# Conditional layer of a fused transformer block: weights standing in array quarters, transposes through the DMA queue of ScalarE, token tiles spread over the long phases

## The chip, the cores and the metric

The kernel runs on one core of a Trainium2 chip. The metric is the device time of one execution in microseconds (us); the lower the better. A time of a kernel is the median of several runs. Beside the times there is one profiled execution, from which all the views below come.

## The reference

The input x is 64 sequences of 64 rows with 1024 columns; 4096 rows in all, called tokens here. The computation is a block of four layers with two residual sums:

```python
W = weights[condition]                       # 16 matrices of 64 x 64, one picked per sequence
y = jnp.einsum('bct,bcd->bdt', x, W)         # conditional layer: mixes the 64 rows of a sequence
x = x + attention(y)                         # 32 heads of 32, qkv projection, softmax over 64, out projection
x = x + ffn(cond2(x))                        # routed low-rank layer, then a quantized gated feed-forward
```

The change concerns the first line alone: for each sequence b, y[b] is the transpose of its 64x64 weight times x[b]. Everything is in float32, apart from the quantized part at the end.

## The kernel before, in words

The kernel has three stages. `attention` does the conditional layer, the qkv projection, scores, softmax and context; the output projection and the second residual stage follow. The change lies in `attention`, which takes about the first 1430 us.

**Blocks and phases.** The 4096 tokens are worked in NBLK = 8 blocks of 512. A block is four tiles of 128 tokens (PB = 4); one tile holds two sequences. For every block the conditional layer's result is kept transposed (columns of x on the partitions), as four quarters named B11, B12, B21, B22 (first index: half of the columns; second: half of the tokens), and from them four differences T1 to T4. These are the operands of a Winograd form of the matrix product, which makes each projection from seven products instead of eight (`Winograd.ORDER` is 1, 6, 7, 5, 2, 4, 3). The projections of a block are four chunks c of query (`psq`) and key (`psk`) rows, seven products of about 1.73 us each, and two groups g of values (`psv`), seven products of 3.45 us each. The work of a block is cut into four phases, one per chunk c. In a phase the scores, the softmax and the context of chunk c are made, while TensorE is filled with the projections of the next chunk ("fills"). Phase 0 holds the query fill, the second values group and the key fill; phases 1 and 2 a query and a key fill; phase 3 the conditional layer of the next block, its first values group and its first query and key fill. So phases 0 and 3 are the long ones.

**Scores to context.** A phase starts two groups of scores (`group`), each of two units u; unit (m, t) is a quarter of the block. A group's 32 passes run on 64x64 quarters of TensorE's array (line 498). The key operand lies in four tiles kbd0 to kbd3, one per unit; kbd1 is written by ScalarE from product 2 (line 419), the others by VectorE (line 421). After the softmax (lines 510 to 522) a unit's probabilities are split into two planes of 16 bits (`parted`, line 528, ScalarE: tile ph), turned by a DMA transpose that SyncE issues (`turned`, line 533: phT), joined again (`joined`, line 540, ScalarE: pT), and used as operand of the context (`context`, line 550). The context's results lie in the PSUM pool `ps_c` of two banks, from which ScalarE copies them (line 561) and sends them away by its own DMA queue (line 562).

**The order of the work.** Each engine works its instructions in the order in which the program issues them, and a semaphore wait holds back all that stands behind it on the same engine. The order is planned by hand: `run` issues a product, lets a clock `now` of planned time go on by its cost, and `at(time, f)` puts a step into a heap from which `run` takes what is due. `rest` parts of products (the copies out of PSUM) are issued one product later (`behind`). `phase` places the two groups at the start and the middle of the phase's planned length. `with_sums` hangs extra VectorE or GpSimd work before a product.

**The conditional layer before** (`conditional`, lines 342 to 381). For a tile j, x is loaded by SyncE (`load_x`, line 246; four at a time for the next block, pool `xp` of 4 buffers), the two 64x64 weights are gathered by GpSimd (line 248) and copied (line 380) into the diagonal of a 128x128 tile `wbd`. TensorE then takes each 128x128 piece of x as the standing operand and streams wbd (line 355): eight matmuls a tile, each two passes in float32, 64 passes a block. This gives y already transposed, in banks of `ps_g` (4 buffers, shared with the projections). VectorE and ScalarE copy in turn (lines 361 and 363) into the quarters; lines 371 and 376 make the T tiles. All of it stands at the start of phase 3, ahead of the products that read it.

**Weights.** Query and key weights are loaded by SyncE into two buffers (line 295, 1.8 MB each): when a projection's last product is issued, the load for the projection after the next one follows. Value weights are seven tiles of 0.5 MB, each loaded after its last use (line 299). `chores`, line 112 and after, prepare weights of the later stages on the side.

Of the kernel before, what the change touches and what calls it, by code (L numbers as in the profile page):

```python
# [182 lines left out]
def attention(tc, a, x_t, ctx_d, ident, dram, ps_g, KC, PB, NBLK, NCH, HPC, H, C, chores, early, op):  # L183
# [27 lines left out]
    with ExitStack() as ctx, ExitStack() as mid:  # L211
# [11 lines left out]
        yp = pool(mid, "y1", 1, side="right")  # L223
        p1 = pool(mid, "p1", 1, side="right")
        w = pool(early, "w1", 1)
        xp = pool(early, "xp", 4)


        cond_i = w.tile([P, KC * 4], I32, tag="cond_i", name="cond_i")
# [6 lines left out]
        nc.vector.tensor_copy(row_f, row_i)  # L236
        nc.vector.tensor_scalar(idx, cond_i, float(C), row_f, ALU.mult, ALU.add)

        def load_x(b):
            tiles = []  # L240
            for j in range(PB):
                i = b * PB + j
                xt = xp.tile([P, H], F32, tag="x", name=f"x_{i}")
                if i == PB - 1:
                    held(xt[:, 0:1], tiles[0][0])
                nc.sync.dma_start(xt, x_t[i])
                wg = xp.tile([P, C], F32, tag="wg", name=f"wg_{i}")
                nc.gpsimd.indirect_dma_start(
                    out=wg[:, :],
                    out_offset=None,  # L250
                    in_=cw,
                    in_offset=bass.IndirectOffsetOnAxis(ap=idx[:, i:i + 1], axis=0),
                )
                tiles.append((xt, wg))
            return tiles

        def held(word, other):


            nc.scalar.copy(word, other[:, 0:1])  # L260
# [24 lines left out]
        def load_qk(b, wh, c, eng=None):  # L285
            t = w_qk[b, wh, c] = wp.tile([P, 7, KQ, P], F32, tag="wqk", name=f"w{wh}_{b}_{c}")
            if b == 0:
                if (wh, c) == ("q", 0):
                    held(t[:, SLOT["A11"], 0, 0:1], x_next[0][1])
                for key in RAW:  # L290
                    nc.sync.dma_start(t[:, SLOT[key], :, :], quarter(key, (0 if wh == "q" else H) + c * P, P))
                return sums(
                    eng or nc.vector, lambda key: t[:, SLOT[key], :, :], lambda: nc.gpsimd.dma_start(qk_d[wh, c], t)
                )
            nc.sync.dma_start(t, qk_d[wh, c])
# [18 lines left out]
            return sums(eng, at, stored)  # L314

        bqkv = act.tile([P, 3 * KC], F32, tag="bqkv", name="bqkv")
        x_next = load_x(0)
        first_sums = load_qk(0, "q", 0) + load_qk(0, "k", 0, nc.gpsimd)
        nc.sync.dma_start(bqkv, a["qkvb_t"])
        first_sums += load_v_raw(0, nc.gpsimd)  # L320
# [1 line left out]

        wbd = []
        for j in range(PB):
            t = w.tile([P, P], F32, tag=f"wbd{j}", name=f"wbd{j}")
            nc.vector.memset(t, 0.0)
            wbd.append(t)
        kbd, vbd = [], []  # L330
        for u in range(4):
            t = act.tile([P, 2, HB], F32, tag=f"kbd{u}", name=f"kbd{u}")
# [6 lines left out]

        B = {}  # L340

        def conditional(b, tiles):

            def one(hf, j):
                key = f"B{hf + 1}{j // 2 + 1}"
                box = []

                def product():
                    xt = tiles[j][0]
                    if j % 2 == 0:  # L350
                        B[key] = yp.tile([P, KQ, HB], F32, tag=key, name=f"y{key}_{b}")
                    ps = ps_g.tile([P, 4, P], F32, tag="g", name=f"cond_{b}_{j}_{hf}")
                    for q in range(KQ):
                        k = hf * KQ + q
                        nc.tensor.matmul(ps[:, q, :], xt[:, k * P:(k + 1) * P], wbd[j], start=True, stop=True)
                    box.append(ps)

                def rest():
                    dst = B[key][:, :, (j % 2) * P:(j % 2 + 1) * P]
                    if j % 2 == 0:  # L360
                        nc.vector.tensor_copy(dst, box[0])
                    else:
                        nc.scalar.copy(dst, box[0])  # L363
                    if (hf, j) == (0, 3):
                        t_of("T1", "B12", "B11")
                    elif (hf, j) == (1, 3):
                        t_of("T2", "B22", "T1")
                        t_of("T3", "B22", "B12")
                    elif (hf, j) == (1, 1):
                        B["T4"] = B["B12"]  # L370
                        nc.vector.tensor_tensor(B["T4"], B["B21"], B["T2"], ALU.subtract)
                return 0.95, product, rest

            def t_of(key, x, y):
                B[key] = yp.tile([P, KQ, HB], F32, tag=key, name=f"{key}_{b}")
                nc.vector.tensor_tensor(B[key], B[x], B[y], ALU.subtract)

            for j, (_, wg) in enumerate(tiles):
                for r in range(2):
                    (nc.gpsimd if b else nc.vector).tensor_copy(wbd[j][halves[r], halves[r]], wg[halves[r], :])  # L380
            return [one(0, j) for j in range(PB)] + [one(1, j) for j in (2, 3, 0, 1)]

        def job(name, cost, n, matmuls, put, begin=None, done=None, order=ORDER):

# [194 lines left out]

        def contexts(least=1):  # L580
            ready = sum(len(pTs) == 2 for *_, pTs in waiting)
            for n in range(ready if ready >= least else 0):
                context(*waiting.pop(0), 1.7 * n * (least - 1))

        def group(b, c, us):


            def begin():
                ps = scores(b, c, us)
                if behind:  # L590
                    behind.pop()()
                contexts(2)
                pTs = []
                waiting.append((b, c, us, pTs))
                for n, u in enumerate(us):
                    at(now + 1.7 * n, lambda n=n, u=u: first(u, ps[n], pTs))
                if b > 0:
                    at(now + 8.7, lambda: next(chores, None))
                    if c in (0, NP - 1):
                        at(now + 15, lambda: next(chores, None))  # L600

            def first(u, ps, pTs):
                p = exponents(b, c, u, ps)
                at(now + 3.4, lambda: normalize(b, c, u, p))
                at(now + 6.8, lambda: second(u, p, pTs))

            def second(u, p, pTs):
                h = parted(b, c, u, p)
                at(now + 1.7, lambda: third(u, turned(b, c, u, h), pTs))

            def third(u, hT, pTs):
                at(now + 8, lambda: pTs.append(joined(b, c, u, hT)))
            return begin
# [63 lines left out]
                with_sums(js, 4, pending_sums, 4)  # L677
            return js

        for f in conditional(0, x_next):  # L680
            run(*f)
        for f in first_sums:
            f()
# [2 lines left out]
        for f in qk_fill(0, 0) + v_fill(0, 0):  # L686
            run(*f)
        for b in range(NBLK):
            if b + 1 < NBLK:
                x_next = load_x(b + 1)  # L690
            for c in range(NP):
                fills, length = [], None
                if c + 1 < NP:
                    fills += qk_fill(b, c + 1)
                    if c == 0:
                        fills[7:7] = v_fill(b, 1)
                        if b == 0:
                            for at_ in range(3, 7):
                                with_sums(fills, at_, v_raw, 1)
                elif b + 1 < NBLK:  # L700

                    fills += conditional(b + 1, x_next) + v_fill(b + 1, 0) + qk_fill(b + 1, 0)
                else:
                    behind.pop()()
                    mid.close()
# [1029 lines left out]
```

## Time and profile before

| what | value |
|---|---|
| median of 3 runs | 2461.12 us (2460.36 to 2464.75) |
| profiled execution, its own time | 2458.5 us |
| span of the profile | 2456.7 us |
| granted TensorE clock, mean | 0.998 |
| TensorE busy in 40:1210 us (blocks 0 to 6 and the change to block 7) | 128.7 to 130 us of each 130 |
| ScalarE busy in the same windows | 44.6 to 59.9 us of each 130 |
| DMA engines busy, share in the same windows | 0.64 to 0.86 |
| DMA transposes of ph | 128, all issued by SyncE |
| DMA packets of ScalarE's queue (q10) | 18432, 16.8 MB, 2.0% of the engines' time |

How to read it: the span is the time from the first to the last instruction in the profile; the execution's own time is a little longer. "Busy" counts instructions that compute; issuing a DMA and waiting do not count. In a timeline, a row is a group of equal instructions with start, duration, engine, source line, operation and tiles; in square brackets stands how long the engine sat idle before, and what released it. PE is TensorE, PEld its weight loads, DVE VectorE, ACT ScalarE, POOL GpSimd, SP SyncE; a q behind an engine's name (SPq, ACTq) is its sequencer, which issues DMAs.

### The profile page before, as it was taken

To read this page: it belongs to the slowest core of one execution; us is meant where nothing else is said; L and a number is where in the kernel's file an instruction comes from. 1 tells how busy PE (TensorE), PEld (TensorE's weight loads), DVE (VectorE), ACT (ScalarE), POOL (GpSimd) and SP (SyncE) were. 2 spreads that over 40 slices of the span, in tenths; PEclk is the share of its full clock that TensorE was granted. 3 is DMA by queue.
4 is the path that set the end of the run, shared out by engine and by line. 5 is a ranking of instruction groups with operands and counts; after the bars stand their busy time and mean duration, and the time that the engine had idled before them with its cause. 6 is when DMAs were issued, how large, how long until landed. Compare 5 with 4: busy or idle time off the path is not lost.

```text
span 2456.7 us, 34195 instructions
## 1 busy us (share of the span) xinstructions
PE 2423.6 (99%) x13194; PEld 1699.7 (69%) x13232; DVE 1532.9 (62%) x2955; ACT 953.2 (39%) x1304; POOL 362.9 (15%) x450
## 2 busy tenths in 40 slices
PE   8999999999999999999999999999999999999997
PEld 7888888888888888888888644444454545445452
DVE  4685585675664755745647633333367777878787
ACT  1343353342443443533434544344423333333333
POOL 5110001011122221210000243433200000000000
PEclk9999999999999999999999999999999999999999
DMA  8894767676677768766646588876744343434343
GB/s 275 286 268 150 219 198 234 189 213 211 199 204 248 202 193 249 206 204 180 176 142 218 175 266 247 268 239 218 235 140 80 88 80 77 89 70 92 74 118 75
DMA packets 419564, 448.07 MB, mean 182 GB/s; under 512 B 300737, under 2 KB 355010, under 8 KB 405698
## 3 DMA queue, kind: packets, MB, share of 16 engines
q1 hardware_dynamic: 388882, 379.21, 52.8%
q0 software_dynamic: 12080, 49.82, 7.6%
q10 hardware_dynamic: 18432, 16.79, 2.0%
q8 instruction: 106, 1.74, 0.3%
q14 instruction: 64, 0.52, 0.1%
HBM read 274.02 MB, written 100.66 MB: 153 GB/s over the span
## 4 chain that ended last, share of the span: by engine, by line
PE 95%; DVE 2%; ACT 1%; DMA 1%; issue 0%; ACTq 0%; SPq 0%; DVEq 0%
PE psva L462 5%; PE pska L435 5%; PE psvd L462 5%; PE psqa L435 5%; PE psvc L462 4%; PE psqc L435 4%; PE pskc L435 4%; PE psqd L435 4%; PE pskd L435 4%; PE pbc L1031 4%; PE pbd L1031 4%; PE pba L1031 4%; PE poa L1031 4%; PE pod L1031 4%; PE poc L1031 4%; PE s L498 3%
## 5 line engine op out<-in xcount | busy, mean ns | idle before, releaser
L540 ACT COPY pT<-phT 128x1024 int16<-128x1024 int16 x128 | 167.2, 1342 | 83.2 <-DMA phT<-ph 83.0
L514 ACT ACTIVATE prob<-prob 128x512 f32<-128x512 f32 x128 | 80.6, 630 | 258.6 <-DVE prob L511 232.4
L421 DVE SCALAR_TENSOR_TENSOR kbd<-pskd,bqkv,psku 32x256 f32<-32x256 f32 x256 | 123.2, 481 | 31.4 <-PE pskd L435 27.6
L528 ACT COPY ph<-prob 128x1024 int16<-128x1024 int16 x128 | 130.7, 1046 | 24.3 <-DVE prob L522 23.7
L1152 POOL TENSOR_TENSOR xo<-xo,ob 128x1024 f32<-128x1024 f32 x32 | 85.0, 2675 | 349.7 <-DVE To L1042 305.5
L561 ACT ACTIVATE co<-c,bqkv 128x256 f32<-128x256 f32 x128 | 60.1, 469 | 179.4 <-PE c L550 152.1
L435 PE MATMUL psqa<-yB,wq 128*128 128x256 f32 x512 | 123.6, 384 | 0.5 <-ACT psqp L406 0.5
L435 PE MATMUL pska<-yB,wk 128*128 128x256 f32 x512 | 122.6, 382 | 0.0
L1538 POOL DMA_DIRECT2D out_dram<-y x29 | 25.2, 869 | 656.2 <-DVE y L1530 644.4
L1126 ACT COPY xh<-xo 128x1024 int16<-128x1024 int16 x64 | 64.0, 1040 | 142.6 <-DVE xo L1171 142.6
L462 PE MATMUL psva<-wv,yB 128*128 128x256 f32 x512 | 117.1, 382 | 0.4
L1031 PE MATMUL poa<-woA,cx 128*128 128x512 f32 x256 | 115.4, 593 | 0.0
L1031 PE MATMUL pba<-wtA,x1T 128*128 128x512 f32 x240 | 107.9, 592 | 0.0
L1137 ACT COPY xTo<-xhT 128x1024 int16<-128x1024 int16 x64 | 84.6, 1338 | 58.4 <-DMA xhT<-xh 51.5
L435 PEld LDWEIGHTS pska<-yB,wk 128*128 128x128 f32 x512 | 96.0, 190 | 15.0 <-issue 2.4
L435 PEld LDWEIGHTS psqa<-yB,wq 128*128 128x128 f32 x512 | 95.1, 190 | 16.0 <-issue 2.8
L462 PEld LDWEIGHTS psva<-wv,yB 128*128 128x128 f32 x512 | 96.1, 190 | 14.4 <-ACT yB L363 1.2
L510 DVE TENSOR_REDUCE mx<-s 128x8 f32<-128x512 f32 x128 | 87.7, 685 | 10.7 <-PE s L498 9.3
L511 DVE TENSOR_TENSOR prob<-s,mx 128x512 f32<-128x512 f32 x128 | 88.5, 691 | 9.3 <-DVE mx L510 0.5
L520 DVE TENSOR_REDUCE den<-prob 128x8 f32<-128x512 f32 x128 | 86.7, 678 | 7.7 <-ACT prob L514 6.9
L522 DVE TENSOR_TENSOR prob<-prob,den 128x512 f32<-128x512 f32 x128 | 88.6, 692 | 4.4
L1031 PEld LDWEIGHTS poa<-woA,cx 128*128 128x128 f32 x256 | 48.4, 190 | 60.1 <-issue 59.7
(251 smaller groups left out, 5140.1 us busy)
## 6 DMA issues: line engine op xcount, KB each, us to landing
wv<-v_d SPq DMA_DIRECT2D x98, 512.0 KB, 4.0
wq<-q_d SPq DMA_DIRECT2D x28, 1792.0 KB, 7.6
wk<-k_d SPq DMA_DIRECT2D x28, 1792.0 KB, 8.1
x<-in_x_dram SPq DMA_DIRECT2D x32, 512.0 KB, 9.2
ctx_d<-co ACTq DMA_DIRECT2D x128, 128.0 KB, 3.9
cx<-ctx_d SPq DMA_DIRECT2D x16, 1024.0 KB, 6.9
xo<-in_x_dram SPq DMA_DIRECT2D x32, 512.0 KB, 5.6
xT_d<-xTo SPq DMA_DIRECT2D x64, 256.0 KB, 3.3
```

What stands on the lines that cost most here:

```text
L421: nc.vector.scalar_tensor_tensor(dst, ps, bias, u, ALU.add, ALU.add)
L435: nc.tensor.matmul(ps[:, 0:HB], A[:, SLOT[A_OF[i]], k, :], B[B_OF[i]][:, k, :], start=first and k == 0, stop=k == KQ - 1, skip_group_check ...
L462: nc.tensor.matmul(ps[:, j * VC:(j + 1) * VC], B[B_OF[i]][:, k, j * P:(j + 1) * P], A[:, k, :], start=first and j == 0 and k == 0, stop=k ...
L510: nc.vector.tensor_reduce(mx_v, ps, AX.X, ALU.max)
L511: nc.vector.tensor_tensor(p.rearrange("p (a e) k -> p a e k", a=2), ps, mx_v.unsqueeze(3).to_broadcast([P, 2, HPC, C]), ALU.subtract)
L520: nc.vector.tensor_reduce(den, p, AX.X, ALU.add)
L522: nc.vector.tensor_tensor(p, p, den.unsqueeze(2).to_broadcast([P, n, C]), ALU.mult)
L528: nc.scalar.copy(h, planes(p.rearrange("p n k -> p (n k)")))
L540: nc.scalar.copy(planes(pT.rearrange("p a b q -> p (a b q)")), hT)
L1031: self.nc.tensor.matmul(ps, self.B[self.B_OF[i]][:, k, :], self.A[self.A_OF[i]][:, k, :], start=first and k == 0, stop=k == self.KQ - 1, s ...
L1137: nc.scalar.copy(planes(xT.rearrange("p k q -> p (k q)")), hT)
L1152: nc.gpsimd.tensor_add(s["x"][:, t, :], s["x"][:, t, :], self.ob)
```

## The change

Block 0 keeps the old form, with its operands in borrowed buffers: two x tiles and one joint `wbd` tile lie in the quarters' buffers. For blocks 1 to 7 the layer is done by tiles, each on its own:

- The gathered 64x64 weights are TensorE's standing operand, and x streams, 512 columns at a time. Four matmuls a tile, one on each 64x64 quarter of the array; the result is not transposed. It lies in both banks of `ps_c`.
- ScalarE splits each half of it into planes of 16 bits (`parted_y`, tile yh), issues a DMA transpose on its own queue (`turned_y`, tile yhT, one buffer), and joins the planes into the quarters (`joined_y`). Planned offsets from the tile's start: 1.7 and 3.4 split, 3.5 and 8.6 transposes, 8.5 and 13.6 joins.
- The quarters of even blocks get buffers of their own, so that they can be written while the block before is still read.
- The tiles of block b + 2 stand in phase 3 of block b (before the fifth product and between the query and the key fill), at the first score group of block b + 1, and in its phase 0 between the second values group and the key fill. For block 1 they stand in phases 0 and 2 of block 0.
- x is loaded two tiles ahead; `xp` has 2 buffers for x and 4 for the weights. The T tiles are made before the last two products of phase 2 and the first two of phase 3.

In the built program the DMA transposes of SyncE and of ScalarE wait for one another: a transpose on one queue waits for the completion of the transposes that were issued before it on the other. Around the key fill of block b's chunk 0, the order is phT of unit 2 (SyncE), yhT (ScalarE), phT of unit 3 (SyncE), yhT (ScalarE). ScalarE's own order there is: split, copy of the first key product, split, issue of yhT, joins pT of units 2 and 3, join of the tile's first half, issue of the second yhT, kbd1. Ahead of the key fill of chunk 1, pT of unit 3 stands behind kbd1.

```diff
-        xp = pool(early, "xp", 4)
+        xp = pool(early, "xp", 2)
...
+            wg = xp.tile([P, C], F32, tag="wg", name=f"wg_{i}", bufs=4)
...
+        def conditional_tile(b, j):
+            xt, wg = x_of.pop((b, j))
+            ps = [ps_c.tile([P, 2, HB], F32, tag="c", name=f"cond{hf}_{b}_{j}") for hf in range(2)]
+            for hf in range(2):
+                for r in range(2):
+                    nc.tensor.matmul(
+                        ps[hf][halves[r ^ hf], :, :], wg[halves[r], :], xt[halves[r], hf * 512:(hf + 1) * 512],
+                        start=True, stop=True,
+                    )
+            if j + 2 < PB:
+                load_x(b, j + 2)
+            elif b + 1 < NBLK:
+                load_x(b + 1, j + 2 - PB)
+
+            def parted_y(hf):
+                h = w.tile([P, 2, 512], I16, tag="yh", name=f"yh_{b}_{j}_{hf}", bufs=2)
+                nc.scalar.copy(h, planes(ps[hf].rearrange("p a t -> p (a t)")))
+                hs[hf] = h
+
+            hs, hTs = {}, {}
+
+            def turned_y(hf):
+                h = hs[hf]
+                hT = w.tile([P, 2, 512], I16, tag="yhT", name=f"yhT_{b}_{j}_{hf}")
+                nc.scalar.dma_start(
+                    hT.rearrange("p h (k q) -> p (h k) q", q=P), h.rearrange("p h t -> p (h t)"), transpose=True
+                )
+                hTs[hf] = hT
+
+            def joined_y(hf):
...
+                for r in range(2) if hf else (slice(0, P),):
...
+                    nc.scalar.copy(dst, src[:, :, :, halves[r] if hf else r])
+
+            for time, f, hf in (
+                (1.7, parted_y, 0), (3.4, parted_y, 1), (3.5, turned_y, 0), (8.5, joined_y, 0), (8.6, turned_y, 1),
+                (13.6, joined_y, 1),
+            ):
+                at(now + time, lambda f=f, hf=hf: f(hf))
...
-                contexts(2)
+                if not contexts(2) and (b, c, us[0]) in tile_groups:
+                    next_tile()
...
+                        for n in (14,) if b else (14, 7):
+                            fills[n:n] = [(0.9, next_tile, None)]
+                    if c + 2 == NP and b + 1 < NBLK:
+                        sums_to_come = [lambda b=b, n=n, Y=Y: t_of(b + 1, Y, *T_OF[n]) for n in range(4)]
+                        with_sums(fills, -2, sums_to_come, 1)
+                        with_sums(fills, -1, sums_to_come, 1)
...
-                    fills += conditional(b + 1, x_next) + v_fill(b + 1, 0) + qk_fill(b + 1, 0)
+                    fills += v_fill(b + 1, 0) + qk_fill(b + 1, 0)
+                    with_sums(fills, 0, sums_to_come, 1)
+                    with_sums(fills, 1, sums_to_come, 1)
...
+                    if b + 2 < NBLK:
+                        tiles_to_come += [(b + 2, j) for j in range(PB)]
+                        for n in (14, 4):
+                            fills[n:n] = [(0.9, next_tile, None)]
```

## The prediction

> **What bounds the kernel now.** I read the page first (shares, chain), then the TensorE timeline at a change of block and in one key projection, then ScalarE's timeline over the same stretch, then the probability tile's transposes.
>
> ```profile
> span 2456.7 us, 34195 instructions
> PE 2423.6 (99%) x13194; PEld 1699.7 (69%) x13232; DVE 1532.9 (62%) x2955; ACT 953.2 (39%) x1304; POOL 362.9 (15%) x450
> ...
> PE 95%; DVE 2%; ACT 1%; DMA 1%; issue 0%; ACTq 0%; SPq 0%; DVEq 0%
> ```
>
> TensorE is busy 99% and carries 95% of the chain that ends last. So a TensorE instruction saved is time saved, and a wait put in front of TensorE is time lost, one for one. Work moved among the other engines costs nothing by its amount; it counts only where TensorE comes to wait for it.
>
> TensorE where block 1 hands over to block 2 (start, us, engine, line, tiles):
>
> ```profile
> 346.23 1.89 PE L435 MATMUL pskd<-yB,wk 128*128 128x256 f32 x8
> 348.05 1.10 PE L498 MATMUL s<-kbd,qT 64*64 64x128 f32 x32
> 349.08 2.08 PE L550 MATMUL c<-pT,vbd 128*64 128x64 f32 x64
> 351.10 7.80 PE L355 MATMUL cond<-wbd,x 128*128 128x128 f32 x64
> 359.02 3.72 PE L462 MATMUL psva<-wv,yB 128*128 128x256 f32 x16
> ```
>
> The conditional layer holds TensorE from 351.10 to 359.02, 7.92 us, with nothing beside it. The score group (32 passes on 64x64 quarters of the array) takes 1.03 us.
>
> TensorE in the first key projection of block 2, ScalarE in the same stretch, and the transposes of ph:
>
> ```profile
> 398.63 1.89 PE L435 MATMUL pska<-yB,wk 128*128 128x256 f32 x8
> ...
> 405.54 1.89 PE L435 MATMUL pska<-yB,wk 128*128 128x256 f32 x8
> 407.27 1.89 PE L435 MATMUL pskc<-yB,wk 128*128 128x256 f32 x8
> 408.99 1.89 PE L435 MATMUL pskd<-yB,wk 128*128 128x256 f32 x8
> 410.81 1.10 PE L498 MATMUL s<-kbd,qT 64*64 64x128 f32 x32
> ```
>
> ```profile
> 400.56 0.37 ACT L406 COPY pskp<-pska 128x256 f32<-128x256 f32 x1 [3.48 <-PE pska L435]
> 400.83 1.34 ACT L540 COPY pT<-phT 128x1024 int16<-128x1024 int16 x1
> 407.47 1.91 ACT L419 ACTIVATE kbd<-pska,bqkv 32x256 f32<-32x256 f32 x4 [5.29 <-PE pska L435]
> ```
>
> ```profile
> L533 SPq DMA_TRANSPOSE phT<-ph x128: 1231/1265/3624, 75.5 to 1418.9; - x128
> ...
> DMA to landing us min/median/max: 3.0/3.6/7.3
> ```
>
> This is the margin to watch. ScalarE copies the key's second quarter (kbd1) out at 407.47, the moment its product is done, and ends at 409.38. The scores read kbd1 from about 411.3, half a microsecond into the group. The margin is 1.9 us. ScalarE works in order, and so far no DMA is waited for in this stretch. A transpose costs its issuer 1.23 to 1.27 us and lands 3.0 to 7.3 us after the issue.
>
> **The change, part by part.**
>
> *Standing weights on quarters.* Out go the 64 passes per block, 7.92 us in block 2, 8.33 in block 1 (178.14 to 186.47, with a wait of 0.74), 7.76 in block 7 (1203.22 to 1210.98): 7 x 7.9 = 55.5 us. (Block 0 keeps its old form.) In come 28 tiles of four 64x64 matmuls with 512 columns, two passes each: 8 x 512 = 4096 columns. That is what a score group streams (32 x 128), on the same four quarters. A score group costs 1.03 us, and about 0.1 each to get in and out (348.05 comes 0.09 after the usual step of 1.73), so a tile is 1.2 us and 28 are 33.6. Gain: **21.9 us**. From below, 1.03 a tile would gain 26.7. From above, since TensorE may wait between the two halves of a tile (each has its own bank), only two quarters run together: 8 passes of 0.43 us by twos is 1.7 us, 1.9 with entry; 53, a gain of 2. I take 1.2, for the score rows are the same form.
>
> *Other engines' amounts.* Out: 28 VectorE copies of 0.68, 28 ScalarE copies of 0.59, 56 GpSimd copies of 0.27. None is on the chain: nothing. In, on ScalarE: 56 splits (row of ph: 1.05), 28 whole joins (row of pT: 1.34), 56 half joins (about 0.75 each), 56 transpose issues of 1.25: 58.8 + 37.5 + 42 + 70 = 208 us in the first 1210, where it is busy 483. It becomes some 56% busy, so its amount hides behind TensorE too. The T subtractions (1.22 each) go to VectorE before products; those ahead of kbd2 and kbd3 delay quarters that are read only half a phase later. The x loads wait for a tile's matmuls in SyncE's queue, and have two tiles' distance to land in (9.2 us); the gathers stand behind GpSimd's casts, with the same distance. One larger memset at the start falls in VectorE's 1.88 us wait for the first gather. All nothing.
>
> *Transposes on a second queue.* Here a rule speaks against the change. By the row alone, each tile's two transposes are 1.25 us of issue and 3.6 of landing, and the planner leaves them 5. But the Trainium skill, "DMA: Bandwidth & Descriptors", section "Silent corruption: two transposing streams in flight at once", says that transposes issued from SyncE and from ScalarE corrupt each other when in flight together, so that the later stream must wait for the earlier one's full completion. No run here shows corruption, but the order of the built program shows the waits. In the first key projection of each block (tile 1 of the next block just ahead) the chain alternates: SyncE's phT of unit 2, ScalarE's yhT, SyncE's phT of unit 3. ScalarE's queue there holds: yh, pskp, yh, issue yhT, pT, pT of unit 3, join, issue yhT, kbd1. So ScalarE waits for a SyncE transpose that waits for ScalarE's own, and kbd1 stands behind it.
>
> First key projection, from its start T (times: rows above; 3.8 from issue to the waiting copy, the median landing and a little): yh and pskp end at 2.3, the second yh at 3.35, yhT issued 3.35, landed 7.2; SyncE issues phT, landed 11.0; pT to 12.3, join to 13.6, second issue to 14.9, kbd1 to 16.8. The scores want it at T + 12.7 (411.3 less 398.6). Stall 4.1 us. Besides, the 1.8 MB query weights are issued about 1 us before T, and such a load takes 7.6 us to land, so the first transpose runs into it; before, transposes stood 7.6 us or more after such loads. I take 4.8, ends 2.9 (landings of 3.0) and 7. By the row alone, without the chain: pT, pT, join, issue from 4.6 end at 9.9, kbd1 at 11.8: no stall.
>
> Second key projection (tile 3 ahead; it comes after a values projection, whose last weight load holds SyncE until TensorE is done, as at 281.18 before): phT of unit 2 lands at T + 3.8, yhT issued then, landed 7.9; join to 9.2; phT of unit 3 landed 11.8; second issue to 13.0; kbd1 to 14.9. Stall 2.3, ends 0.2 and 4.
>
> Query projection between (tile 2): the same chain ends with the qT copy at about 14.8 after its start; TensorE needs that bank only at the second product of the values projection after it, at 15.5: 0, ends 0 and 1.5. Tile 0, in the values projection: products of 3.45 us cover it: 0.
>
> Block 0: three tiles lie within 25 us, and the chain of six transposes ends ahead of kbd1 once more: 3, ends 1 and 5.
>
> The first two stalls come six times (tiles of blocks 2 to 7): 6 x (4.8 + 2.3) + 3 = **45.6 us** lost, ends 20 and 80.
>
> **Sum.** -21.9 + 45.6 = +23.7. The profiled execution took 2458.5 us (span 2456.7 and 1.8 around it), giving 2482; the median of the runs is 2.6 higher, giving 2484.8, say 2484.
>
> **Rivals.**
> - *ScalarE keeps up* (the other side). Landings near 3.0 us and copies that run earlier than worked out here would leave the margin before kbd1 unspent. Mechanism: only TensorE's passes count. Price 21.9 less some 3 in block 0: 2442. For it: before, ScalarE waited up to 7.1 us for phT without a stall on TensorE worth naming. Against it: those waits lay in values projections, not ahead of kbd1. It decides if the two stalls together stay under 3.1 us a block: 6 x 3.1 + 3 = 21.6.
> - *Even.* Both chains at landings of 3.0: 6 x (2.9 + 0.2) + 1 = 19.6 against 21.9: 2459.
> - *Quarters by twos.* If the waits between the halves of a tile part the passes, the gain is 2 and the stalls stay: 2461 + 44 = 2505. Against it: the score passes start four at a time, though there too tiles wait.
> - *Transposes into loads.* Landings of 5 to 7 us in both chains: 6 x (7 + 4) + 5 = 71 lost, net +49: 2510.
>
> **How the numbers follow.** Forecast 0.50; ScalarE keeps up 0.20; even 0.10; by twos 0.08; into loads 0.12. Five microseconds, 0.2%, is about what a measurement of this kernel can tell from no change. Faster: all of the second and a fifth of the even case, 0.22. Same: most of the even case, 0.08. Slower: 0.70. The range goes from the keeping-up case to just beyond the loads case, 2440 to 2518. Of the signs, slower holds most; its own range is 2467 to 2518.
>
> **What would show it.** Right: L396 (the tile) busy about 1.0 us each and no L355-like block of 7.9 us between blocks; on TensorE a new wait "s <- ACT kbd1" of 4 to 6 us in the first and 2 to 3 us in the second key projection of each block; on ScalarE waits of pT for phT right before it. Wrong: TensorE still at 99% with a shorter span (keeping up); tile rows of 1.9 us (by twos); stalls on "psvb" or "psqb" rather than on s (a bank, not the key); waits of tiles for x or wg (the loads I cost at nothing).

## The result and the profile after

The changed kernel takes 2550.36 us, median of 6 runs (2540.55 to 2552.92); the kernel before, run beside it, 2461.38 (2460.36 to 2464.75). The ratio is 1.036, with a 95% interval of 1.035 to 1.0371: slower by 89 us, where the prediction had 23 and a range up to 2518. The direction was right, the size was not.

The profiled execution took 2552.92 us (span 2551.0), 94.3 more in span than the one of before. Span, busy times, granted clock and the chain's shares on the page after:

```profile
span 2551.0 us, 33874 instructions
PE 2439.3 (96%) x12970; PEld 1667.8 (65%) x13008; DVE 1511.5 (59%) x2924; ACT 1062.1 (42%) x1416; POOL 347.9 (14%) x394
PEclk9889999999999999999999999999999999999999
PE 77%; DMA 8%; ACT 3%; DVE 2%; issue 1%; ACTq 1%; SPq 0%; POOL 0%; DVEq 0%; POOLq 0%
```

TensorE has left 99%: the chain that ends last now runs 8% through DMA (it had 1%) and 77% through TensorE (95%). TensorE is busy 15.7 us *more* than before, although the change takes work away from it: that is the first sign that its rows have become slower, and the clock row's 8s in the second and third slice are the second. TensorE's waits after (engine, line, what it waited for; us in total, times, longest):

```profile
PE s L559 <- ACT kbd L480: 48.1, 25, 15.0
PE cond L396 <- ACT yh L407: 21.8, 1, 21.8
```

To place this, I cut TensorE's rows at the first values product of each block (block 7: to the last context) and compared lengths and idle time:

```
block            0      1      2      3      4      5      6      7
before, us     142.5  172.5  170.2  170.1  170.6  170.4  170.7  216.7
after, us      187.4  184.5  176.9  181.9  176.9  176.7  174.9  218.9
more idle       40.7   10.2    5.5    6.9    5.2    4.9    4.3    2.2
tile passes     -1.5   -2.6   -2.4   -2.4   -2.5   -2.4   -2.6    0.0
other passes    +5.6   +4.6   +3.5   +7.1   +3.9   +3.9   +2.7   +0.5
```

Block 0 alone makes half of the loss. In blocks 1 to 6 there is more idle time, and besides each block's unchanged passes take 3 to 7 us longer than before.

Block 0, TensorE's and ScalarE's timelines (idle before a row, and its releaser, in brackets):

```profile
104.19 3.62 PE L523 MATMUL psvd<-wv,yB 128*128 128x256 f32 x16
129.64 3.40 PE L396 MATMUL cond<-x,wg 64*64 64x512 f32 x8 [21.83 <-ACT yh L407]
...
148.97 0.67 PE L559 MATMUL s<-kbd,qT 64*64 64x128 f32 x16
164.60 0.68 PE L559 MATMUL s<-kbd,qT 64*64 64x128 f32 x2 [14.97 <-ACT kbd L480]
```

```profile
82.42 1.36 ACTq L415 DMA_TRANSPOSE yhT<-yh  x1
...
105.73 1.35 ACT L429 COPY yB<-yhT 128x1024 int16<-128x1024 int16 x1 [17.68 <-DMA yhT<-yh]
107.11 1.30 ACTq L415 DMA_TRANSPOSE yhT<-yh  x1
126.82 1.38 ACT L429 COPY yB<-yhT 128x512 int16<-128x512 int16 x2 [19.74 <-DMA yhT<-yh]
128.07 0.61 ACT L575 ACTIVATE prob<-prob 128x512 f32<-128x512 f32 x1
128.60 0.99 ACT L407 COPY yh<-cond 128x1024 int16<-128x1024 int16 x1
```

ScalarE issues the first transpose at 82.42 and can join it at 105.73; it issues the second at 107.11 and joins it at 126.82. While it stands there, its copy of the next tile's result (yh) stands behind, both banks of ps_c stay full, and the third tile waits 21.8 us on TensorE. The DMA records say what the transposes met: each is 1024 packets of 256 bytes. Alone (the one issued at 139.9) they take 1.4 us from first to last. The first took 20.1 us, with 433 packets of GpSimd's queue (6.3 KB on average, up to 14 KB: the stores of the combined weights, L292 and L312) and 746 of SyncE's between them, 579 of these raw weight loads of 512 bytes; the second took 17.6 us, with 408 and 280. Packets of others are not all of it: in the second, 327 of the transpose's own packets took over 0.1 us each (up to 2.6), where one takes 0.018 alone. These make about half of its time (its packets add up to 9.2 us of all 16 engines, to 1.4 for one that runs alone), and no run here shows what slowed them.

A later block, around the key projection that starts at 456.48; TensorE, ScalarE, and SyncE's queue:

```profile
468.76 0.67 PE L559 MATMUL s<-kbd,qT 64*64 64x128 f32 x16
473.62 0.68 PE L559 MATMUL s<-kbd,qT 64*64 64x128 f32 x2 [4.20 <-ACT kbd L480]
...
477.36 3.10 PE L496 MATMUL psqa<-yB,wq 128*128 128x256 f32 x8
480.30 1.89 PE L496 MATMUL psqb<-T,wq 128*128 128x256 f32 x8
```

```profile
458.57 1.37 ACTq L415 DMA_TRANSPOSE yhT<-yh  x1
...
468.70 1.34 ACT L601 COPY pT<-phT 128x1024 int16<-128x1024 int16 x1 [7.37 <-DMA phT<-ph]
469.91 1.31 ACT L429 COPY yB<-yhT 128x1024 int16<-128x1024 int16 x1
471.25 1.33 ACTq L415 DMA_TRANSPOSE yhT<-yh  x1
472.63 1.91 ACT L480 ACTIVATE kbd<-pska,bqkv 32x256 f32<-32x256 f32 x4 [1.40 <-issue]
```

```profile
464.87 1.24 SPq L594 DMA_TRANSPOSE phT<-ph  x1
```

This is the chain of the prediction: ScalarE's transpose (458.57, landed after 6.3 us), only then SyncE's (464.87), the copy that waits for it 7.37 us, join, second issue, kbd1. The scores wait 4.20 us. And then the query's first product takes 3.10 us where its kind takes 1.99 (the key's first product at 456.48): the granted clock is recorded as one half from 472.8 to 479.6.

### The profile page after: what moved, and what is told of

The parts are those of the page before. It is cut to its first block, busy times and chain, and to the rows that moved or that the text cites. A ratio compares the mean times of both kernels' runs of the same rounds, so it can differ in the third digit from the quotient of the medians.

```text
span 2551.0 us, 33874 instructions
## 1 busy us (share of the span) xinstructions
PE 2439.3 (96%) x12970; PEld 1667.8 (65%) x13008; DVE 1511.5 (59%) x2924; ACT 1062.1 (42%) x1416; POOL 347.9 (14%) x394
## 4 chain that ended last, share of the span: by engine, by line
PE 77%; DMA 8%; ACT 3%; DVE 2%; issue 1%; ACTq 1%; SPq 0%; POOL 0%; DVEq 0%; POOLq 0%
DMA yhT<-yh 4%; PE pbc L1112 4%; PE pbd L1112 4%; PE pba L1112 4%; PE poa L1112 4%; PE pod L1112 4%; PE poc L1112 4%; PE psqa L496 4%; PE psqd L496 4%; PE psqc L496 3%; PE psva L523 3%; DMA phT<-ph 3%; PE psvd L523 3%; PE psvc L523 3%; PE pska L496 3%; PE pr L1381 2%
## 5 line engine op out<-in xcount | busy, mean ns | idle before, releaser
L589 ACT COPY ph<-prob 128x1024 int16<-128x1024 int16 x128 | 129.8, 1043 | 14.8 <-DVE prob L583 12.1
L496 PE MATMUL psqa<-yB,wq 128*128 128x256 f32 x512 | 130.8, 400 | 2.0 <-ACT psqp L467 2.0
L559 PE MATMUL s<-kbd,qT 64*64 64x128 f32 x2048 | 84.2, 286 | 48.1 <-ACT kbd L480 48.1
L429 ACT COPY yB<-yhT 128x512 int16<-128x512 int16 (+1 forms) x84 | 76.3, 952 | 94.3 <-DMA yhT<-yh 93.9
L559 PEld LDWEIGHTS s<-kbd,qT 64*64 64x64 f32 x2048 | 60.3, 137 | 76.9 <-ACT kbd L480 55.2
```

What stands on the lines that cost most here:

```text
L496: nc.tensor.matmul(ps[:, 0:HB], A[:, SLOT[A_OF[i]], k, :], B[B_OF[i]][:, k, :], start=first and k == 0, stop=k == KQ - 1, skip_group_check ...
L559: nc.tensor.matmul(ps[halves[r], hp, n, jj * 2:(jj + 1) * 2, :], q_of[b, c][halves[hp], m, t * HB + t0:t * HB + t0 + C], kbd[u][halves[hp] ...
L589: nc.scalar.copy(h, planes(p.rearrange("p n k -> p (n k)")))
```

## The experiments

Each run was timed beside the kernel before on the same chip. "Block 0", "blocks 1 to 6" are lengths cut as above (before: 142.5 and 1024.5; after: 187.4 and 1071.8).

**1. No transposes of yh** (the conditional outputs of blocks 1 to 7 come out unturned).

```diff
             def turned_y(hf):
                 h = hs[hf]
+                if True:
+                    hTs[hf] = h
+                    return
```

> The changed kernel without the 56 transposes of yh: each join copies the untransposed halves, so the conditional outputs of blocks 1 to 7 lie in the wrong order (values differ, work is otherwise the same: tiles, splits, joins, loads). Theory A (ScalarE waits in its queue for transposes, with kbd1, yh and the bank copies behind them): every new stall goes and with them the lowered clock; 2461 less the 16 to 22 us that the tiles save: 2440 to 2446. Rival B (the amount of ScalarE's copies, or the tiles' own cost, is what TensorE waits for): stalls on kbd1 stay, 2475 or more.

Measured: 2439.52 us against 2457.71, ratio 0.993 (0.9913 to 0.9947). Block 0 138.1, blocks 1 to 6 1007.1; TensorE has less than 1 us more idle time than before in all blocks together, and the clock is 0.998. So TensorE waits for none of the tiles' splits, joins, loads and gathers; the tiles' own gain is 20.9 us of span. All of the loss, 115 us between the two profiles, comes with the transposes: 49.3 in block 0, 64.7 in blocks 1 to 6.

**2. None in block 1's tiles** (the same edit with `if b == 1`; block 1's outputs unturned).

> Transposes of yh left out for the tiles of block 1 alone (its conditional outputs lie in the wrong order), which run in block 0; blocks 2 to 7 keep theirs. Theory A1 (block 0 loses 45 us because its transposes land 20 us late among the stores of the combined weights): block 0 back to its old length, 2500 to 2508. Rival A2 (the same chain of waits in every block, block 0 no worse by its place): saves what a later block loses, about 8: 2540 to 2545.

Measured: 2497.19, ratio 1.0163 (1.0146 to 1.018). Block 0 137.9, blocks 1 to 6 1066.4. The loss of block 0 is its own tiles' transposes, and carries little into later blocks.

**3. Transposes of yh by SyncE**.

```diff
-                nc.scalar.dma_start(
+                nc.sync.dma_start(
                     hT.rearrange("p h (k q) -> p (h k) q", q=P), h.rearrange("p h t -> p (h t)"), transpose=True
```

> The transposes of yh issued by SyncE instead of ScalarE, so that all transposes are on one queue in order and none waits for the landing of one on another queue. Theory C (the waits across the two queues make the chain too long): blocks 1 to 6 lose 0 to 10 us together instead of 47, block 0 still loses 20 or more to late landings among stores: 2480 to 2510. Rival D (slow landings, not the waits across queues, make the stalls; ScalarE still waits in its order): 2530 to 2555. SyncE now waits for yh with weight loads behind it, which could show as TensorE waiting for wk or wv.

Measured: 2465.61, ratio 1.0037 (1.0024 to 1.0049): better than the theory had it. Blocks 1 to 6 1019.2, shorter than before the change; block 0 152.1, 9.6 longer than before. One word of the change, the issuing engine, holds over 80 of its 89 us. In SyncE's queue a transpose stands in order with the loads: block 1's transposes now take 1.4 to 4.7 us from first to last packet, with at most 34 packets of SyncE's loads between their own (707 and 256 for the two above). But the first of them is no earlier than in the changed kernel. SyncE issues it at 96.08, where ScalarE did at 82.42, and the join waits as long (17.78 us here, 17.68 there); it is the second that comes early (111.59 against 126.82):

```profile
96.08 3.86 SPq L415 DMA_TRANSPOSE yhT<-yh  x1
```

```profile
107.09 1.34 ACT L429 COPY yB<-yhT 128x1024 int16<-128x1024 int16 x1 [17.78 <-DMA yhT<-yh]
111.59 1.38 ACT L429 COPY yB<-yhT 128x512 int16<-128x512 int16 x2 [3.16 <-DMA yhT<-yh]
```

The one word changes three things at once: the waits across queues, what the transposes run beside, and 56 issues of 1.25 us that ScalarE no longer pays.

**4. kbd1 copied by VectorE.**

```diff
+                    if u is None:
+                        nc.vector.tensor_scalar(
+                            kT[rows, h % 2, :], ps[rows, :], bqkv[rows, KC + ch:KC + ch + 1], None, ALU.add
+                        )
+                        continue
                     biased(kT[rows, h % 2, :], ps[rows, :], bqkv[rows, KC + ch:KC + ch + 1], u and u[rows, :])
```

> The kbd1 copies go to VectorE (same arithmetic), all else as changed. Theory E (only kbd1 stands behind the chain): the 37 us of waits on kbd1 and the low clock after them go in blocks 1 to 6, and the 15 us wait in block 0: 2485 to 2500, with the 21.8 us wait of a tile for yh left. Rival F (the next ScalarE copy, pskp, psqp or qT, takes its place): waits on psqa, psqb or s<-qT of 2 to 4 us a block, 2515 to 2540.

Measured: 2542.46, ratio 1.0363 (1.0331 to 1.0394): beyond even the rival's 2515 to 2540. TensorE's waits in this run:

```profile
PE psqa L496 <- ACT psqp L467: 38.7, 9, 7.6
PE cond L396 <- ACT yh L407: 21.1, 1, 21.1
```

The wait on kbd1 is gone and another of the same size stands in its place, on a bank that ScalarE has not emptied. ScalarE is late as a whole, and TensorE waits for whichever of its copies it needs first.

**5. The kernel before, with ScalarE held up** by copies of 0.63 us ahead of kbd1, one dose a block.

```diff
...
+                    if u is None and h == 0 and 1 <= c <= 2 and b < NBLK - 1:
+                        for _ in range(3 + b if c == 1 else 10 + 2 * b):
+                            nc.scalar.copy(idle, idle)
                     biased(kT[rows, h % 2, :], ps[rows, :], bqkv[rows, KC + ch:KC + ch + 1], u and u[rows, :])
```

> The kernel before, with idle ScalarE copies of 0.63 us put ahead of kbd1, 3 to 9 of them in the second phase of blocks 0 to 6 and 10 to 22 in the third: waits of TensorE for kbd1 of about 0 to 4 us and 4 to 12 us, one dose a block, nothing else changed. Theory G (a wait of TensorE of over some 3 us lowers its granted clock for a few us after it): the matmuls after the longer waits take longer, 2 to 4 us a wait, by whatever cause it waits; under about 3 us none. Rival H (the low clock belongs to the changed kernel, its quarter matmuls or its transfers): every other row keeps its length and the clock stays 1.00.

Measured: 2529.91 (one run). The doses made one gap a block of 2.5, 3.8, 5.1, 6.4, 7.7, 9.0 and (with one of 1.6) 10.3 us; the other passes of these blocks took 3.4, 2.5, 2.6, 3.1, 2.9, 3.8 and 4.8 us longer. Around the gap of block 1:

```profile
329.15 0.69 PE L503 MATMUL s<-kbd,qT 64*64 64x128 f32 x2 [3.83 <-ACT kbd L421]
330.12 1.12 PE L503 MATMUL s<-kbd,qT 64*64 64x128 f32 x14 [0.28 <-ACT kbd L421]
331.17 3.62 PE L555 MATMUL c<-pT,vbd 128*64 128x64 f32 x64
334.72 1.99 PE L437 MATMUL psqa<-yB,wq 128*128 128x256 f32 x8
```

The context's 64 passes take 3.62 us; in the prediction's rows they took 2.08. The same, in windows (TensorE and its clock stand in the third and the third-last column):

```profile
300.00:325.00 25.00, 25.00 (x153) 21.47 (x155) 20.94 (x40) 14.22 (x20) 1.15 (x2) 1.00 0.62 194
329.00:336.00 7.00, 6.57 (x86) 5.64 (x87) 2.81 (x5) 2.78 (x7) 0.00 (x0) 0.60 0.48 189
336.00:360.00 24.00, 24.00 (x139) 20.83 (x138) 17.30 (x34) 13.99 (x20) 3.03 (x10) 1.00 0.49 141
```

So here a wait of 2.5 us or more costs TensorE its length and about 3 us more, in a kernel without any of the change. The recorded clock accounts for most of that: half of the work time that lies in its half-clock spells is 3.2, 2.6, 2.1, 2.7, 2.6, 3.1 and 4.1 us in these blocks. How long a wait must be is not sharp. Counted over blocks 0 to 6 of all 18 traces, a half-clock spell began within or up to 5 us after each of the 78 waits of 3.2 us and more, 15 of the 20 from 2.0 to 3.2 us, and 8 of the 25 from 1.0 to 2.0. The Trainium skill, "TensorE: Matmul & The Clock Gate", Part 1, states such a gate, half rate after an idle window of about 3.4 us; the traces agree for the longer waits and show half clock after many shorter ones too.

**6. The changed kernel with extra copies by GpSimd beside tile 1's first transpose**, 0, 1, 2, 4, 7, 10 copies of 0.5 MB at blocks 2 to 7.

```diff
...
                 hTs[hf] = hT
+                if hf == 0 and j == 1:
+                    for n in range({3: 1, 4: 2, 5: 4, 6: 7, 7: 10}.get(b, 0)):
+                        nc.gpsimd.dma_start(spare[n], ...)
```

> The changed kernel with 0 to 10 copies of 0.5 MB from an input to a spare buffer, issued by GpSimd right after the first transpose of tile 1 of blocks 2 to 7 (0, 1, 2, 4, 7 and 10 copies). Theory I (a transpose on its own queue lands late when another queue moves large packets): the wait of ScalarE for that yhT grows with the dose, from some 6 us to 15 to 25 us at 7 and 10, and TensorE's wait with it, as in block 0. Rival J (block 0 is late by its chain of waits, not by traffic): the waits stay as they are, 3 to 5 us a block.

Measured: 2571.15 (one run). TensorE's wait for kbd1 was 3.3, 5.0, 3.3, 3.9, 6.1 and 11.4 us. The yhT join came no later than before (10 to 12 us after the issue), for the copies had gone out ahead of it and had landed. At the largest dose they met the transpose of ph before it, whose packets took 10.8 us with 834 of GpSimd's packets between them, and yhT was issued late. TensorE's wait grows at the two largest doses, but by another transpose than the theory named; run 13 repeats it.

**7. All transposes by ScalarE** (those of ph too: `nc.sync` to `nc.scalar` in `turned`).

> All transposes, those of ph too, issued by ScalarE: no transpose waits for one on another queue, but all are on a queue apart from the loads, and ScalarE pays 128 more issues of 1.25 us. Theory C (waits across queues are what hurts): stalls of blocks 1 to 6 mostly go, 2490 to 2520, block 0 still late. Theory I (transposes on a queue of their own land late beside loads on another): phT lands late as well, 7 to 12 us where before it took 3.6, and the time is 2545 or more.

Measured: 2535.21, ratio 1.0302 (1.0269 to 1.0335), between the two. Block 0 178.7, with 15.7 and 16.3 us for the packets of the first two transposes: without any wait across queues block 0 gives back only 9 of its loss. Blocks 1 to 6 1053.6, 18 less than the change: there the waits across the queues are part of the loss, and that they are all of it is not shown. (A further 6 us go in block 7, where run 15, with the same issues on ScalarE, loses 7.)

**8. By SyncE, with block 1's four tiles behind the stores.**

```diff
-        tile_groups = [(0, 0, 2), (0, 2, 0)] + [(b, 0, 0) for b in range(1, NBLK - 1)]
+        tile_groups = [(b, 0, 0) for b in range(1, NBLK - 1)]
...
-                        for n in (14,) if b else (14, 7):
+                        for n in (14,):
                             fills[n:n] = [(0.9, next_tile, None)]
+                    if b == 0:
+                        for n in ((), (9, 2), (2,))[c]:
+                            fills[n:n] = [(0.9, next_tile, None)]
```

> Transposes of yh by SyncE as in the run before, and the four tiles of block 1 moved from the first phase of block 0 to after its stores (one late in the first phase, two in the second, one in the third). Theory (block 0 loses only by its place among the stores and by tiles close together): block 0 ends 2 to 4 us shorter than before the change, in all 2448 to 2456, faster than before. Rival (SyncE, waiting for yh with loads behind it, keeps the loss): 2460 to 2468.

Measured: 2471.88, ratio 1.0064 (1.0047 to 1.0081), slower than run 3: the theory missed. Block 0 156.3, with gaps of 3.5 and 7.1 us on kbd1: in the later phases the steps of the tiles stand right around kbd1 in ScalarE's order, and the transposes stand in SyncE's queue among raw weight loads in packets of 512 bytes (L290).

**9 and 10. By SyncE with later joins; and with one of block 1's tiles moved.**

```diff
-                (1.7, parted_y, 0), (3.4, parted_y, 1), (3.5, turned_y, 0), (8.5, joined_y, 0), (8.6, turned_y, 1),
-                (13.6, joined_y, 1),
+                (1.7, parted_y, 0), (3.4, parted_y, 1), (3.5, turned_y, 0), (8.5 if b == 1 else 11, joined_y, 0),
+                (8.6 if b == 1 else 11.1, turned_y, 1), (13.6 if b == 1 else 17, joined_y, 1),
```

(Run 10 besides drops the 7 of `(14, 7)` and puts that tile at place 2 of phase 1.)

> Transposes of yh by SyncE, and the joins of blocks 2 to 7 put 2.5 and 3.4 us later in ScalarE's order (11 and 17 us after the tile instead of 8.5 and 13.6), so that ScalarE finds the transposed tile landed. Theory (what is left of the stalls in blocks 1 to 6 is ScalarE waiting for yhT in its order): their sum falls by 3 to 8 us against SyncE's transposes alone: 2457 to 2463. Rival (what is left is not that wait, or a later join pushes the second transpose into kbd1's time): 2465 or more.

> As the run with later joins, and of block 1's tiles the first is taken out of the 16 us in which block 0 stores its combined weights: one beside each score group as before, one late in the first phase, one early in the second. Theory (block 0's loss comes from three tiles among the stores): block 0 loses 2 us or less instead of 9.6, 2449 to 2456, the same as before or a little faster. Rival (its raw weight loads of 512-byte packets hold SyncE's transposes anywhere in block 0, as in the run with all four moved): 2460 to 2470.

Measured: 2458.18, ratio 0.9991 (0.9984 to 0.9998), and 2457.56, 0.9988 (0.9981 to 0.9995), both against 2460.47. Blocks 1 to 6 fall to 1012.0 and 1011.8, near the 1007.1 of run 1: most of what was left there was ScalarE asking too early. Block 0 stays at 152.5 and 151.4: moving one tile did not cure it.

**11. The change as it is, by ScalarE, with block 1's tiles moved as in run 8.**

> The changed kernel, transposes by ScalarE, with block 1's four tiles moved behind the stores of block 0 (one late in the first phase, two in the second, one in the third). Theory A1 (45 us of the loss are transposes landing among block 0's stores): block 0 loses 10 to 25 us, as other stalls on kbd1 come in: 2515 to 2532. Rival A2 (block 0 loses by the chain of waits wherever its tiles lie): 2540 or more.

Measured: 2538.61, ratio 1.0312 (1.0273 to 1.035). Block 0 181.5: away from those 16 us of stores it loses only 6 us less. The second transpose now took 12.6 us, beside 172 packets of 10.8 KB (query weights being stored) and 864 of 0.5 KB (raw loads). Block 0 has such traffic all along.

**12. Run 10 with kbd1 by VectorE.**

> As the run with later joins and block 1's tiles moved, and kbd1 copied by VectorE. Theory (with ScalarE no longer far behind, taking kbd1 off it removes the last stalls on s without moving them to the bank copies): 2 to 5 us less than without it, 2445 to 2453, faster than before. Rival (the waits move to psqa and pska as they did with ScalarE's transposes): no gain or slower than without it.

Measured: 2463.89, ratio 1.0014 (1.0007 to 1.0021): the rival. Block 0 160.0, with waits of 1.1 and 5.1 us on psk's bank and of 6.5 us on a bank of ps_c that ScalarE had not emptied.

**13 and 14. The doses of run 6, aimed**: GpSimd first reads a word of yh, so its copies go out with the transpose; 1, 2, 4, 7, 10 copies at the tiles of blocks 3 to 7.

```diff
...
                 hTs[hf] = hT
+                if hf == 0 and j == 1 and b > 2:
+                    nc.gpsimd.tensor_copy(seen_h, h[:, 0, 0:2])
+                    for n in range((1, 2, 4, 7, 10)[b - 3]):
+                        nc.gpsimd.dma_start(spare[n], ...)
```

> The changed kernel with copies of 0.5 MB in packets of 4 KB, input to spare buffer, issued by GpSimd once yh of tile 1 is split, beside its first transpose: 1, 2, 4, 7 and 10 copies at blocks 3 to 7. Theory I1 (queues take turns packet by packet, so a transpose's 1024 packets of 256 bytes each wait for a packet of the other queue): that transpose lands later by some 1.4 us a copy, up to 10 to 13 us. Rival I2 (queues share by bytes): it lands later by 1 to 2 us whatever the dose. Rival J: no change.

> The same copies, the same bytes, in packets of 512 bytes. Theory I1 (turns packet by packet): the transpose lands later by 2 to 3 us at most, for a 512-byte packet takes about 0.03 us where one of 4 KB took 0.16, and the larger doses add nothing. Rival I2 (shared by bytes): the same as with packets of 4 KB.

Measured, run 13 (2574.42, one run), for that transpose's 1024 packets, by copies beside it:

```
copies                               0      1      2      4      7     10
first to last packet, us           1.9    3.2    4.1    8.1   11.7   12.8
packets of the copies in between     0    105    249    528   1028   1185
TensorE's wait for kbd1, us        4.2    5.3    6.1    9.8   13.7   16.0
```

(At 4 and 7 copies some 470 packets of SyncE's queue, of 512 bytes, lay in between as well.) The transpose is 0.26 MB; at 7 copies 3.7 MB went by before it was through. That is no sharing by bytes. Up to 7 copies nearly all that was sent passed in between, so these sums alone do not show the turns; the packets' times do. With 10 copies the two queues keep step: in each us from 1187 to 1197 went 66 to 108 packets of the transpose and 62 to 108 of the copies, never more than 5 apart, and a packet of the copies took 0.16 us (median), one of the transpose 0.018. It is turn by turn, about one packet for one, and it ends when the transpose's 1024 are spent. With 10 copies, ScalarE:

```profile
1182.22 1.38 ACTq L417 DMA_TRANSPOSE yhT<-yh  x1
...
1204.29 1.33 ACT L607 COPY pT<-phT 128x1024 int16<-128x1024 int16 x1 [19.30 <-DMA phT<-ph]
...
1208.13 1.91 ACT L486 ACTIVATE kbd<-pska,bqkv 32x256 f32<-32x256 f32 x4 [1.33 <-issue]
```

The Trainium skill, "DMA: Bandwidth & Descriptors", section "Queues, rings and completion order", says that an engine goes round its queues by packets; these counts agree, if a record of the trace is what that page calls a packet, which no run here shows. Run 14 (2582.21, one run) tells nothing of packet size: its copies went out in packets of 3.6 KB as well, and its numbers are those of run 13 (11.8 and 12.8 us at 7 and 10 copies).

**15. The kernel before, with its own transposes (ph) by ScalarE.**

> The kernel before with its own transposes, those of ph, issued by ScalarE: one queue for all transposes, so no waits across queues, but a queue apart from the loads; none of the change's tiles. Theory I (a transpose queue apart from the loads lands late beside other traffic): phT lands 10 to 20 us late in block 0 among its stores and raw loads, and block 0 loses 10 to 40 us; later blocks lose little. Theory C (only waits across two transposing queues hurt): within 10 us of the kernel before.

Measured: 2468.65 (one run). Blocks 0 to 5 are as before, within 0.4 us each: theory I's 10 to 40 us in block 0 missed. phT landed up to 12.1 us after its issue, but TensorE's idle time in these blocks did not change. The 10 us went at the end of the stage (blocks 6 and 7). So a queue of its own for transposes did no harm in six of the blocks. It is a weak test of block 0, though: its transposes there met next to none of GpSimd's stores (36 packets of that queue beside one of them).

**16. Run 10 with the later joins for block 1 too.**

> Transposes of yh by SyncE, block 1's tiles moved, and the later joins in all blocks, block 1's tiles too (before: blocks 2 to 7). Theory (what block 0 still loses, 8.9 us, is ScalarE waiting in its order for late yhT with kbd1 behind): block 0 loses 2 to 5, in all 2449 to 2455. Rival (the transposes land later than any such lag among block 0's raw loads): no gain on 2457.

Measured: 2454.49 against 2460.17, ratio 0.998 (0.997 to 0.9989). Block 0 147.1, blocks 1 to 6 1014.0. This version is 0.2% faster than the kernel before: a small gain, though its interval excludes none. It is under a third of what run 1 shows the tiles to be worth.

## Why the prediction missed

It named the place of the waits in the later blocks rightly, and a chain that the trace shows there; it missed two terms that make most of the loss. Span by span: forecast -21.9 + 42.6 + 3 = +23.7; measured -20.9 (run 1) + 64.7 + 49.3, and 1.2 elsewhere, = +94.3.

- *Standing weights on quarters, gain 21.9.* Right: 20.9 by run 1 (21.8 in blocks 0 to 6, less some 2 that block 7 takes longer). Tile rows are 1.04 to 1.23 us each there, not 1.9, so "quarters by twos" falls. In the changed kernel 21 of 28 are 1.04 to 1.09; six of 2.33 and one of 3.40 lie in half clock. (The sum has slips too small to matter: 7 x 7.9 is 55.3, and the 8.33 includes a wait of 0.74.)
- *Other engines' amounts, nothing.* Right (run 1): less than 1 us of idle in all.
- *First key projection, 4.8 a block.* Right: gaps of 4.2, 4.2, 4.3, 3.6, 3.8 and 3.1 us on kbd1, in each ScalarE waiting 6.0 to 7.4 us for phT just before. With the small gaps behind them 25.4 us in all, where 28.8 was forecast.
- *Second key projection, 2.3 a block.* Too much: 0.5 to 2.2 us a block, 7.4 in all, where 13.8 was forecast. Idle time in blocks 1 to 6 is 37.0 more than before, where 42.6 was forecast; the two come this near in part by luck, for some 4 us of the 37.0 are waits on ps_c and psqa that the prediction did not have.
- *A wait costs its length, "one for one".* This failed. TensorE is slower after it: against run 1, the passes of blocks 1 to 6 take 27.5 us more, for 9 gaps of 1.6 to 4.3 us there; half of the work time in their recorded half-clock spells is 20 us of it. Run 5 makes the same 3 us a gap without the change. The term was missing from the sum, and the profile of before could not show it: from 44 to 1426 us its longest gap on TensorE was 0.74 us.
- *"Block 0: three tiles lie within 25 us, and the chain of six transposes ends ahead of kbd1 once more: 3, ends 1 and 5."* This is the step that failed most: 49.3 us, 41.9 of it idle. I gave these transposes 3.8 us from issue to the waiting copy. The first two took 23.3 and 19.7 us to the join, beside block 0's stores of combined weights and raw loads. Run 13 shows how packets of others stretch a transpose, by turns; for half of the second one's time, its own slow packets, the cause stays open. The landing statistics I leaned on were of transposes in SyncE's queue, in line with its loads. In that line (run 3) block 0 loses 14.0 us against run 1 instead of 49.3, although its first tile is joined no earlier. And the first wait was not on kbd1 but on yh and the banks of ps_c.
- *The rule on two transposing streams.* Its waits are in the trace (464.87 above), and cost time in blocks 1 to 6. How much of their 64.7 us is those waits and how much slow landings on a queue apart isn't settled: run 7 takes the waits away and gives back 18, but adds issues to ScalarE; run 3 takes both away, and 56 issues of ScalarE besides, one of which stands right ahead of kbd1, and gives back 53. No run moves those issues alone.
- *Rivals.* "Transposes into loads" came nearest and had the right kind of cause, but priced block 0 at 5 us of the 49.3, since it looked at the two key projections of the later blocks. "ScalarE keeps up" (2442) is the limit that run 1 shows without any transposes of yh (2439.5).

## What to carry to other kernels

Before a small-packet transfer is put on a queue of its own, look at what the other queues move at that moment: its landing time in an ordered queue says little of its landing beside someone else's large packets. A start-up block with its own stores and raw loads needs its own estimate. And price a new wait of TensorE of over about 2 us at its length plus some 3 us of slow clock: here half clock followed 15 of 20 waits of 2.0 to 3.2 us and every longer one.

## What the runs showed of the hardware

- 1024 transposed packets of 256 bytes took 1.4 us alone, 11.7 to 12.8 us beside 1000 and more packets of 3.6 KB, 20.1 us beside 433 packets of stores of 6.3 KB on average and 746 of loads.
- In run 5 a TensorE gap of 2.5 to 9.0 us was followed by half clock for 6.8 to 10.2 us as recorded (the spells begin within the gap or just before its end) and by 2.5 to 3.8 us of lost time, nearly independent of the gap's length. In all traces the recorded spells in blocks 0 to 6 are multiples of about 3.4 us (3.4, 6.8, 10.2 and more).
